# Position network: channels sorted by the sign of their last weight, four keys a group, half sums added by an accumulating DMA

## The chip, the cores and the metric

The kernel runs on one core of a Trainium2 chip. The core has a matrix engine (TensorE, PE in the profile; its weight loads are PEld), three other compute engines (VectorE, DVE; ScalarE, ACT; GpSimd, POOL), a sync engine (SP) and 16 DMA engines. Matmul results go to PSUM, everything else lives in SBUF (128 partitions) or in DRAM. All data are f32. The metric is the time of one execution on the device, in microseconds (us), median of several runs.

## The reference

Four layers follow each other on an image tensor; only the first is touched by the change, a deformable attention layer on x of shape (2, 512, 32, 32) with 8 heads. Its bias on the attention scores comes from a small network (the position network) that is evaluated for every pair of a query position (1024 of them) and a sampled key position (64 for each of 2 x 8 = 16 image and head pairs):

```python
pos = grid_q[:, :, None, :] - grid_kv[:, None, :, :]          # (16, 1024, 64, 2)
bias = jnp.sign(pos) * jnp.log1p(jnp.abs(pos))
bias = jax.nn.relu(bias @ cpb_w1 + cpb_b1)                    # 2 -> 128
bias = jax.nn.relu(bias @ cpb_w2 + cpb_b2)                    # 128 -> 128
bias = (bias @ cpb_w3 + cpb_b3).reshape(b, GROUPS, H * W, Hd * Wd)   # 128 -> 1
sim = jnp.einsum('bhid,bhjd->bhij', qh, kh) + bias
attn = jax.nn.softmax(sim, axis=-1)
out = jnp.einsum('bhij,bhjd->bhid', attn, vh)
```

The middle layer alone is 16 x 64 x 1024 columns through a 128 x 128 matrix. After this layer come an output projection, an MLP, a deformable convolution layer, a linear attention layer and a plain attention layer.

## The kernel before

The queries, keys and values are made first (`queries_keys_values`, L618 to L824): depthwise convolution of q on PE and DVE (L582, L591), the sampled positions, and the sampled features as matmuls (L788). Its results are q in a padded buffer that lies in a large buffer called room, the keys as two-head blocks `kbd`, and the signed logarithms of the distances, stored to DRAM as `feat`.

Then the position network runs (`biased_scores`, L827). The 16 image and head pairs go in eight steps of two (index p), each step over its keys. The hidden channels (128) stand on the partitions, the 1024 queries along the free dimension. The first layer is separable in x and y: `first_layer` (L510) loads the tables `ab` from `feat` by SP, and ACT scales them (L533). For a key, `hidden` adds a row of the x table and a column of the y table on DVE (L868) into a tile `h1` of 128x1024, and a ReLU follows in place, on ACT (L877) or, for 3 keys of 16, on DVE (L875). The pool of `h1` has six buffers.

The second layer goes by two keys (`second_layer`, L880). PE works in four column strips of 32: each of the two PSUM tiles `ph` gets 32 output channels of each key twice over, so that the lower 64 channels of both keys lie in the first tile and the upper 64 in the second. ACT evacuates the first with a ReLU (`lo`, L898), the second with a ReLU of the channels scaled by the size of their last weight (`hi`, L900); DVE adds `lo` times a signed quotient (`low_w`) to `hi` (L901). The last layer (L909) multiplies the sums by a matrix of signs, 128x32, that collects two keys; eight matmuls serve four pairs, and the result builds up in a PSUM tile `sim` over the 16 steps of a p. The scores q times k are added into the same PSUM tile by PE (`scores`, L921). `store` (L931) copies `sim` plus the last bias to the table simT. There are three PSUM tiles for `ph`.

PE's queue has the order of the program text. The queues of DVE, ACT, POOL and SP are put in order at build time by a scheduler that goes by the program text and by when it expects an operand; an engine executes its queue strictly in that order. An instruction waits for the semaphores of what it reads, and of the last readers of what it overwrites.

In the second half of the stage (p of 4 and more) the softmaxes of the first image's four steps are woven in (L1005 to L1032). The MLP's first weights (4 MB) and the output weights are loaded by SP in the middle of the last p (`load_weights`, L317), into the buffer that held q. After the stage come the projection (L1055, L1067) and the MLP (L1127, L1116).

Of the kernel before, what the change touches and what calls it, by code (L numbers as in the profile page):

```python
# [17 lines left out]
C = 512  # L18
CC = 4
HW = 1024  # L20
NP = 8
# [51 lines left out]
def constants():  # L73
    p = np.arange(128)
    px, py = (p % 32).astype(np.float32), (p // 32).astype(np.float32)
    neg_y = np.stack([-(py + 4.0 * c) for c in range(8)], axis=1).astype(np.float32)
    j = np.arange(64)
    gx, gy = (j % 8).astype(np.float32), (j // 8).astype(np.float32)

    gj = np.stack([gx, gy]).reshape(2, 1, 4, 16).repeat(16, axis=1)  # L80
    gj = gj.transpose(2, 0, 1, 3).reshape(128, 16)
    line = (2.0 * np.arange(32, dtype=np.float32) / np.float32(31) - 1.0).astype(np.float32)
    groups = np.zeros((128, 128), np.float32)
    for g in range(8):
        groups[16 * g : 16 * g + 16, 16 * g : 16 * g + 16] = 1.0 / 16

    y, x = np.divmod(np.arange(HW), 32)
    taps = np.zeros((HW, 9, 2), np.float32)
    for k in range(9):
        taps[:, k, 0] = y + k // 3 - 1  # L90
        taps[:, k, 1] = x + k % 3 - 1
    taps = taps.reshape(8, 128, 18).transpose(1, 0, 2).reshape(128, 144)
    parts = [
        ("ident", np.eye(128, dtype=np.float32)),
        ("groups", groups),
        ("minus", np.broadcast_to(np.array([0.0, -1.0], np.float32), (128, 2))),
        ("neg_xh", -px[:, None] - np.float32(0.5)),
        ("neg_yh", neg_y - np.float32(0.5)),
        ("gx", np.broadcast_to(gx, (128, 64))),
        ("gy", np.broadcast_to(gy, (128, 64))),  # L100
        ("gj", gj),
        ("line", np.broadcast_to(line, (128, 32))),
    ]
    packed, at = _pack(parts)
    return packed, at, taps


def layouts(i):
# [10 lines left out]
    for name in ("cpb_b2", "cpb_w3"):  # L119

        halves = np.asarray(i["L0_conv_" + name]).reshape(2, 64, 1)
        parts.append((name, np.concatenate([_twice(halves[0]), _twice(halves[1])], axis=1)))
# [20 lines left out]
    cst, cst_at, taps = constants()  # L143
# [8 lines left out]
    for h in range(2):  # L152
# [17 lines left out]
        "w2": np.asarray(i["L0_conv_cpb_w2"]),  # L170
# [106 lines left out]
def layers(net, out):  # L277
# [12 lines left out]
    with ExitStack() as later:  # L290
# [12 lines left out]
        with ExitStack() as l0a:  # L303
# [8 lines left out]
            w2 = keys.tile([128, 128], F32, name="w2_t", tag="w2")  # L312
            first = net.pool(l0a, "cpb_ab", 4)
            parts = queries_keys_values(net, bn, simT, q_flat, q_pad, kbd, val, feat, first)
            nc.sync.dma_start(out=w2, in_=net.ins["w2"])

            def load_weights():  # L317
                t = new_room()
                w1 = t[:, : 4 * 2048].rearrange("p (k m) -> p k m", m=2048)
                out_w = t[:, 4 * 2048 :].rearrange("p (k m) -> p k m", m=C)  # L320
                nc.sync.dma_start(out=out_w, in_=net.ins["out_w"])
                nc.sync.dma_start(out=w1, in_=net.ins["mlp_w1"])
                return w1, out_w

            w1, out_w = biased_scores(
                net, q_pad, kbd, feat, w2, simT, first, parts, load_weights
            )

# [289 lines left out]
def queries_keys_values(net, bn, simT, q_flat, q_pad, kbd, val, feat, first):  # L618
# [5 lines left out]
    with ExitStack() as ctx:  # L624
# [15 lines left out]
        with ExitStack() as part:  # L640
# [33 lines left out]

            pd = bank("pd")
# [6 lines left out]
            nc.scalar.activation(g, g, AF.Gelu, bias=net.vec("odw_b"))  # L682

        with ExitStack() as part:
# [61 lines left out]

            for gt, name in grids:
                g3 = gt.rearrange("p (n j) -> p n j", j=64)
                base = net.cst(name).unsqueeze(1).to_broadcast([128, NP, 64])
                nc.vector.scalar_tensor_tensor(g3, g3, 4.0, base, ALU.mult, ALU.add)  # L750
# [55 lines left out]
            for w, out, factor in ((kw, kbd, 64**-0.5), (vw, val, 1.0)):  # L806
                for q in range(2):
# [15 lines left out]
                    )  # L823
    return done  # L824


def biased_scores(net, q_pad, kbd, feat, w2, simT, first, parts, load_weights):  # L827
# [12 lines left out]
    with ExitStack() as ctx:  # L840
        small = net.pool(ctx, "cpb_w", 1)
        hid1 = net.pool(ctx, "cpb_h1", 6)
        lows = net.pool(ctx, "cpb_lo", 2)
        highs = net.pool(ctx, "cpb_hi", 6)
        ps_h = net.psum(ctx, "cpb_ps_h", 3)
        ps_sim = net.psum(ctx, "cpb_ps_sim", 1)
        w3_lo, w3_hi = net.vec("cpb_w3", 0), net.vec("cpb_w3", 1)
        b2_lo, b2_hi = net.vec("cpb_b2", 0), net.vec("cpb_b2", 1)
        sign = small.tile([128, 1], F32, name="sign", tag="sign")
        nc.vector.tensor_scalar(sign, w3_hi, 0.0, 2.0, ALU.is_ge, ALU.mult)  # L850
        nc.vector.tensor_scalar(sign, sign, 1.0, None, ALU.subtract)
        size = small.tile([128, 1], F32, name="size", tag="size")
        nc.vector.tensor_tensor(size, w3_hi, sign, ALU.mult)
        size_b = small.tile([128, 1], F32, name="size_b", tag="size_b")
        nc.vector.tensor_tensor(size_b, size, b2_hi, ALU.mult)
        low_w = small.tile([128, 1], F32, name="low_w", tag="low_w")
        nc.vector.tensor_tensor(low_w, w3_lo, sign, ALU.mult)

        w3 = small.tile([128, 62], F32, name="w3", tag="w3")
        nc.vector.memset(w3, 0.0)  # L860
        nc.vector.tensor_copy(w3[0:64, 30:31], sign[0:64, :])
        nc.vector.tensor_copy(w3[64:128, 31:32], sign[64:128, :])

        def hidden(i, j, on_vector):
            at_x, at_y = parts[i, j % 32 // 16]
            k = 16 * (j // 32) + j % 16
            h1 = hid1.tile([128, HW], F32, name="h1", tag="h1")
            nc.vector.tensor_tensor(  # L868
                h1.rearrange("p (y x) -> p y x", x=32),
                at_x[:, k : k + 1, :].to_broadcast([128, 32, 32]),  # L870
                at_y[:, k, :].unsqueeze(2).to_broadcast([128, 32, 32]),
                ALU.add,
            )
            if on_vector:
                nc.vector.tensor_scalar(h1, h1, 0.0, None, ALU.max)  # L875
            else:
                nc.scalar.activation(h1, h1, AF.Relu)  # L877
            return h1

        def second_layer(pair):  # L880

            phs = []
            for k in range(2):
                ph = ps_h.tile([128, HW], F32, name="ph", tag="ph")
                for n in range(2):
                    for t in range(4):
                        c0 = 64 * k + 32 * (t % 2)
                        nc.tensor.matmul(  # L888
                            ph[32 * t : 32 * t + 32, half(n)],
                            lhsT=w2[:, c0 : c0 + 32],  # L890
                            rhs=pair[t // 2][:, half(n)],
                            start=True,
                            stop=True,
                            skip_group_check=True,
                        )
                phs.append(ph)
            lo = lows.tile([128, HW], F32, name="lo", tag="lo")
            nc.scalar.activation(lo, phs[0], AF.Relu, bias=b2_lo)  # L898
            hi = highs.tile([128, HW], F32, name="hi", tag="hi")
            nc.scalar.activation(hi, phs[1], AF.Relu, bias=size_b, scale=size)  # L900
            nc.vector.scalar_tensor_tensor(hi, lo, low_w, hi, ALU.mult, ALU.add)  # L901
            return hi

        def last_layer(sim, j, sums):


            for n in range(2):
                for t in range(4):
                    nc.tensor.matmul(  # L909
                        sim[32 * t : 32 * t + 32, half(n)],  # L910
                        lhsT=w3[:, 30 - j : 62 - j],
                        rhs=sums[t][:, half(n)],
                        start=(j == 0),
                        stop=(j == 30),
                        skip_group_check=True,
                    )

        def scores(p, sim):
            for n in range(2):
                for t in range(2):  # L920
                    nc.tensor.matmul(  # L921
                        sim[64 * t : 64 * t + 64, half(n)].rearrange("p (y x) -> p y x", x=32),
                        lhsT=kbd[:, p, 64 * t : 64 * t + 64],
                        rhs=q_pad[:, p, 1 + 16 * n : 17 + 16 * n, 1:33],
                        start=False,
                        stop=False,
# [3 lines left out]
        def store(p, sim):  # L930
            nc.vector.tensor_scalar(simT[:, p, :], sim, net.vec("cpb_b3"), None, ALU.add)  # L931
# [16 lines left out]
        hidden_done = 0  # L948
        for p, j in [(p, j) for p in range(NP) for j in range(0, 32, 2)]:
# [5 lines left out]
            for t in range(4):  # L955
                pair = []
                for k in range(2):
                    key = j + 32 * (t % 2) + k
                    pair.append(hidden(2 * p + t // 2, key, hidden_done % 16 in (3, 8, 13)))
                    hidden_done += 1  # L960
                sums.append(second_layer(pair))
# [6 lines left out]
            elif j == 16:  # L968
                scores(p, sim)
                if p == NP - 1:  # L970
                    weights = load_weights()
# [7 lines left out]
        return weights  # L979
# [1184 lines left out]
```

## Time and profile before

| what | value |
|---|---|
| three runs | 3840.08, 3830.84, 3836.54 us, median 3836.54 |
| profiled execution, first to last instruction (the page gives no other time of it) | 3835.8 us |
| busy: PE, weight loads, DVE, ACT, POOL | 3739.0, 1487.3, 2765.5, 2566.4, 189.1 us |
| second layer of the position network (L888), first and last start | 86.6 and 2116.4 us |
| L888 matmuls, records | 16384, 593 ns each, 1808.0 us in all |
| ACT ReLU of h1 (L877); evacuations L898 and L900 | 872.1; 571.8 and 621.3 us |
| DVE first-layer sums (L868); additions (L901) | 1206.0; 654.8 us |

How to read it: an f32 matmul shows as two records; four of them run side by side in the four strips, so that the sum of their durations is four times the time they take. The mean of a group includes the end of the instruction that overlaps with the next one's start; the distance between the starts of two instructions that follow each other is shorter. Idle time of an engine counts only where that engine is what the others wait for.

### The profile page before, as it was taken

Reading aid. Unit: us, or ns where it says so; the run is one execution under the profiler, and the core shown is the slowest. Engines: PE = TensorE matmul, PEld = TensorE weight load, DVE = VectorE, ACT = ScalarE, POOL = GpSimd, SP = SyncE. Lnnn points to the kernel's source line nnn. Section 1 sums busy time; section 2 is a strip of 40 time slices with the busy share of each in tenths; the row PEclk is TensorE's granted clock in tenths of the full one; section 3 lists DMA queues with packets and bytes.
Section 4 is the critical chain, followed back from the end, with each engine's and each line's share of the span. In section 5 each row is a group of like instructions: output and inputs, shape, how many; then the busy total and the mean of one; then the engine's idle time right before and its main releaser. Section 6 shows DMA issues by size and latency. Waiting matters only on the chain. (4 is left out here: it accounts for less than half of the span.)

```text
span 3835.8 us, 59384 instructions
## 1 busy us (share of the span) xinstructions
PE 3739.0 (97%) x25356; PEld 1487.3 (39%) x25356; DVE 2765.5 (72%) x3242; ACT 2566.4 (67%) x2941; POOL 189.1 (5%) x180
## 2 busy tenths in 40 slices
PE   7999999999999999999999999999979999899999
PEld 4532222223222322232323444444434544455555
DVE  6999999999999999999999210411475472566565
ACT  7999999999999999999999221211123243345544
POOL 0000000000000000000000000000261150000000
PEclk9999999999999999999999999999999999999999
DMA  3000000000000000000000100112455481000000
GB/s 111 1 23 23 23 1 23 23 23 12 12 23 23 12 12 23 23 12 12 23 23 34 61 0 0 40 61 77 143 185 173 140 276 42 1 12 1 1 20 25
DMA packets 54459, 168.57 MB, mean 44 GB/s; under 512 B 4804, under 2 KB 10436, under 8 KB 51252
## 3 DMA queue, kind: packets, MB, share of 16 engines
q1 hardware_dynamic: 31556, 83.77, 6.2%
q0 software_dynamic: 21776, 79.14, 6.2%
q8 instruction: 200, 3.28, 0.4%
q10 hardware_dynamic: 864, 1.86, 0.2%
q14 instruction: 63, 0.52, 0.0%
HBM read 156.11 MB, written 8.65 MB: 43 GB/s over the span
## 5 line engine op out<-in xcount | busy, mean ns | idle before, releaser
L888 PE MATMUL ph<-h,w_t 128*32 128x512 f32 x16384 | 1808.0, 593 | 15.7 <-ACT lo L898 6.5
L868 DVE TENSOR_TENSOR h<-ab 128x1024 f32<-128x1024 f32 x1024 | 1206.0, 1219 | 67.2 <-PE ph L888 66.2
L888 PEld LDWEIGHTS ph<-h,w_t 128*32 128x32 f32 x16384 | 547.6, 110 | 1239.9 <-issue 1017.2
L877 ACT ACTIVATE h<-h 128x1024 f32<-128x1024 f32 x832 | 872.1, 1067 | 45.6 <-DVE h L868 42.9
L901 DVE SCALAR_TENSOR_TENSOR hi<-lo,low_w,hi 128x1024 f32<-128x1024 f32 x512 | 654.8, 1279 | 31.6 <-ACT hi L900 30.3
L900 ACT ACTIVATE hi<-ph,size_b,size 128x1024 f32<-128x1024 f32 x512 | 621.3, 1214 | 16.7 <-PE ph L888 12.5
L898 ACT ACTIVATE lo<-ph,vec_t 128x1024 f32<-128x1024 f32 x512 | 571.8, 1117 | 5.8 <-PE ph L888 5.4
L2086 ACT ACTIVATE e<-pl,m 128x1024 f32<-128x1024 f32 x128 | 143.6, 1122 | 228.9 <-DVE m L2078 228.9
L1567 PE MATMUL po<-fold,turned 128*128 128x512 f32 x576 | 266.1, 606 | 3.2 <-DVE dfacc L1575 2.9
L2078 DVE TENSOR_REDUCE m<-pl 128x1 f32<-128x1024 f32 x128 | 150.7, 1219 | 147.2 <-PE pl L1988 147.2
L1135 ACT ACTIVATE h<-ph,vec_t 128x512 f32<-128x512 f32 x64 | 44.0, 687 | 312.0 <-PE ph L1127 311.5
L909 PE MATMUL sim<-hi,w 128*32 128x512 f32 x2048 | 251.0, 592 | 0.0
L1127 PE MATMUL ph<-xn,room 128*128 128x512 f32 x512 | 230.9, 594 | 0.0
L1116 PE MATMUL acc<-h,mlp_w_t 128*128 128x512 f32 x512 | 229.8, 592 | 0.0
L1514 DVE SCALAR_TENSOR_TENSOR sum<-got,wts,sum 128x256 f32<-128x256 f32 x432 | 184.4, 478 | 48.8 <-ACT sum L1510 46.4
L1490 POOL DMA_INDIRECT got<-table,idx x144 | 175.0, 1215 | 554.9 <-DVE sum L1514 268.0
L2040 PE MATMUL pt<-cst_t,e 128*128 128x128 f32 x1024 | 149.3, 279 | 6.6 <-ACT aT L2051 4.0
L2040 PEld LDWEIGHTS pt<-cst_t,e 128*128 128x128 f32 x1024 | 118.6, 142 | 93.6 <-issue 61.3
L1567 PEld LDWEIGHTS po<-fold,turned 128*128 128x128 f32 x576 | 106.6, 195 | 112.4 <-issue 107.4
L1116 PEld LDWEIGHTS acc<-h,mlp_w_t 128*128 128x128 f32 x512 | 97.3, 190 | 122.5 <-issue 122.0
L1127 PEld LDWEIGHTS ph<-xn,room 128*128 128x128 f32 x512 | 96.6, 191 | 117.7 <-issue 117.1
L1541 ACT COPY turned<-pt 128x512 f32<-128x512 f32 x72 | 41.9, 582 | 143.8 <-PE pt L1535 143.6
(250 smaller groups left out, 2711.6 us busy)
## 6 DMA issues: line engine op xcount, KB each, us to landing
ab<-feat_d SPq DMA_DIRECT2D x64, 512.0 KB, 4.0
room<-in_dc_w_dram SPq DMA_DIRECT2D x9, 1024.0 KB, 4.8
dc_w_t<-in_dc_w_dram SPq DMA_DIRECT2D x5, 1024.0 KB, 5.3
room<-in_mlp_w_dram SPq DMA_DIRECT2D x1, 4096.0 KB, 15.6
mlp_w_t<-in_mlp_w_dram SPq DMA_DIRECT2D x1, 4096.0 KB, 12.5
dc_w_t<-in_dc_w_dram SPq DMA_DIRECT2D x8, 512.0 KB, 5.0
w_qkv_t<-in_w_qkv_dram SPq DMA_DIRECT2D x3, 1024.0 KB, 8.6
out_dram<-x_all SPq DMA_DIRECT2D x12, 256.0 KB, 2.0
```

The lines of the kernel that those rows point to most:

```text
L868: nc.vector.tensor_tensor(h1.rearrange("p (y x) -> p y x", x=32), at_x[:, k : k + 1, :].to_broadcast([128, 32, 32]), at_y[:, k, :].unsquee ...
L877: nc.scalar.activation(h1, h1, AF.Relu)
L888: nc.tensor.matmul(ph[32 * t : 32 * t + 32, half(n)], lhsT=w2[:, c0 : c0 + 32], rhs=pair[t // 2][:, half(n)], start=True, stop=True, skip_ ...
L898: nc.scalar.activation(lo, phs[0], AF.Relu, bias=b2_lo)
L900: nc.scalar.activation(hi, phs[1], AF.Relu, bias=size_b, scale=size)
L901: nc.vector.scalar_tensor_tensor(hi, lo, low_w, hi, ALU.mult, ALU.add)
L909: nc.tensor.matmul(sim[32 * t : 32 * t + 32, half(n)], lhsT=w3[:, 30 - j : 62 - j], rhs=sums[t][:, half(n)], start=(j == 0), stop=(j == 30 ...
L1116: nc.tensor.matmul(accs[oc], lhsT=self.w2[:, m, 128 * oc : 128 * oc + 128], rhs=hs[m], start=(m == 0), stop=(m == 15),)
L1127: nc.tensor.matmul(ph, lhsT=self.w1[:, k, 128 * m : 128 * m + 128], rhs=xn[:, k, :], start=(k == 0), stop=(k == CC - 1),)
L1514: nc.vector.scalar_tensor_tensor(t[:, q, :], g[:, s, :], w, t[:, q, :], ALU.mult, ALU.add)
L1567: nc.tensor.matmul(self.out, lhsT=turned[:, at : at + 128], rhs=self.folded.w[k][:, i, :], start=(k == 0 and i == 0), stop=(k == 8 and i = ...
L2040: nc.tensor.transpose(pt[:, 128 * c : 128 * c + 128], e[:, 128 * k : 128 * k + 128], ident)
```

## The change

The 128 channels of the second layer are sorted on the chip (class `Order`) by the sign of their last weight, into four quarters of 32, such that each lane's quarters can be combined with one sign per lane. The weights of the second layer are scaled by the size of the last weight and permuted by matmuls with 0/1 matrices; biases, signs and one constant are put in the same order. These are some 70 DVE instructions on single columns, mostly, a few tiny matmuls and two small loads.

`biased_scores` then works by four keys: `hidden` makes two keys at once (128x2048) in one of four places of the buffer room (the place of the MLP's weights, and of q before that); one ReLU pair in 16 is on DVE (L1021 of the changed kernel), the others on ACT (L1023). A PSUM tile holds one quarter of the channels for four keys. ACT evacuates three quarters (L1042), DVE adds the first two (L1051), and takes the fourth from PSUM while adding the third (L1055: max with the negative bias, the rest of the ReLU going into the constant). The second of these half sums is added to the first by an accumulating DMA from SBUF to SBUF on POOL's queue (L1056). The last layer takes four keys at once, so it runs half as often. The scores are computed for all p before the stage and stored in simT; `store` adds them. The output weights are loaded before the stage, the MLP's after it.

```diff
+            t = new_room()
+            w1 = t[:, : 4 * 2048].rearrange("p (k m) -> p k m", m=2048)
...
+            nc.sync.dma_start(out=out_w, in_=net.ins["out_w"])
+            biased_scores(net, feat, order, simT, first, parts, w1)
+            for k in range(4):
+                nc.sync.dma_start(out=w1[:, k, :], in_=net.ins["mlp_w1"][:, k, :])
...
+class Order:
...
+    def ranks(self, tmp, room, bank):
...
+        nc.vector.tensor_scalar(self.plus, w3, 0.0, None, ALU.is_ge)
...
+        nc.vector.tensor_scalar(self.turned, self.turned, size, None, ALU.mult)
...
+        for n, lhsT in enumerate((self.at[:, 128:256], self.ones)):
+            nc.tensor.matmul(pr[:, n : n + 1], lhsT=lhsT, rhs=self.plus, start=True, stop=True)
...
+    def places(self, pr):
...
+        scalar(
+            self.spread,
...
+            up,
+            None,
+            ALU.is_equal,
+        )
+
+    def put(self, bank):
...
+        nc.scalar.copy(self.w2, pw[:, :128])
...
+    def constant(self, bank):
...
@@ def queries_keys_values
+            ranks = order.ranks(w, val.rearrange("p n m -> p (n m)"), bank)
             pd = bank("pd")
...
+            order.places(ranks)
...
+            order.put(bank)
+            order.constant(bank)
...
+            for p in range(NP):
+                for n in range(2):
+                    pq = bank("pqk")
+                    for t in range(2):
+                        nc.tensor.matmul(
+                            pq[64 * t : 64 * t + 64, :].rearrange("p (y x) -> p y x", x=32),
+                            lhsT=kbd[:, p, 64 * t : 64 * t + 64],
+                            rhs=q_pad[:, p, 1 + 16 * n : 17 + 16 * n, 1:33],
...
+                    (nc.vector.tensor_copy, nc.scalar.copy)[n](simT[:, p, half(n)], pq)
...
@@ def biased_scores
-        hid1 = net.pool(ctx, "cpb_h1", 6)
-        lows = net.pool(ctx, "cpb_lo", 2)
-        highs = net.pool(ctx, "cpb_hi", 6)
+        lows = net.pool(ctx, "cpb_lo", 4)
+        adds = net.pool(ctx, "cpb_add", 3)
+        highs = net.pool(ctx, "cpb_hi", 7)
...
-        def hidden(i, j, on_vector):
+        def hidden(i, j, at, on_vector):
...
-            h1 = hid1.tile([128, HW], F32, name="h1", tag="h1")
+            h1 = room[:, at, :].rearrange("p (k i) -> p k i", k=2)
             nc.vector.tensor_tensor(
...
-        def second_layer(pair):
...
+        def quarter(quad, q):
+            ph = ps_h.tile([128, HW], F32, name="ph", tag="ph")
+            for n in range(2):
+                for t in range(4):
+                    nc.tensor.matmul(
+                        ph[32 * t : 32 * t + 32, half(n)],
+                        lhsT=order.w2[:, 32 * q : 32 * q + 32],
+                        rhs=quad[t][:, half(n)],
...
+        def rectified(ph, q):
+            t = lows.tile([128, HW], F32, name="lo", tag="lo")
+            nc.scalar.activation(t, ph, AF.Relu, bias=order.bias[:, q : q + 1])
+            return t
+
+        def second_layer(quad):
+            r0 = rectified(quarter(quad, 0), 0)
+            r1 = rectified(quarter(quad, 1), 1)
+            total = highs.tile([128, HW], F32, name="hi", tag="hi")
+            nc.vector.scalar_tensor_tensor(total, r0, order.low, r1, ALU.mult, ALU.add)
+            r2 = rectified(quarter(quad, 2), 2)
+            ph = quarter(quad, 3)
+            more = adds.tile([128, HW], F32, name="more", tag="more")
+            nc.vector.scalar_tensor_tensor(more, ph, order.floor, r2, ALU.max, ALU.add)
+            nc.gpsimd.dma_start(out=total, in_=more, accum_op=ALU.add)
+            return total
...
-        for p, j in [(p, j) for p in range(NP) for j in range(0, 32, 2)]:
+        for p, j in [(p, j) for p in range(NP) for j in range(0, 32, 4)]:
...
             for t in range(4):
-                pair = []
-                for k in range(2):
+                quad = []
+                for k in range(0, 4, 2):
                     key = j + 32 * (t % 2) + k
-                    pair.append(hidden(2 * p + t // 2, key, hidden_done % 16 in (3, 8, 13)))
-                    hidden_done += 1
-                sums.append(second_layer(pair))
+                    quad += hidden(2 * p + t // 2, key, pairs_done % 4, pairs_done % 16 == 7)
+                    pairs_done += 1
+                sums.append(second_layer(quad))
                 if t == 1 and pending is not None:
                     last_layer(sim, *pending[1:])
```

## The prediction

> **What bounds the kernel now.** I read the page first (busy shares, the 40 slices), then the busy time by stretches, then the groups of instructions inside the position network, then its order in time. In the slices the first 55% of the span has PE, DVE and ACT all at nine tenths. The line table puts the first L888 matmul at 86.6 us and the last at 2116.4 us: the position network holds 2030 of the 3835.8 us. A stretch from its middle (length, then busy time of PE, weight loads, DVE, ACT and POOL, granted clock, DMA share, GB/s), and its groups over 1000 us:
>
> ```profile
> 600.00:1000.00 400.00, 397.25 (x3664) 117.65 (x3660) 379.57 (x344) 389.85 (x382) 0.00 (x0) 1.00 0.05 17
> ```
>
> ```profile
> L888 PE MATMUL ph<-h,w_t 128*32 128x512 f32 x8071 | 890.0, 593 | 6.9 <-ACT lo L898 3.7 <-ACT hi L900 2.4 <-DVE h L875 0.8
> L868 DVE TENSOR_TENSOR h<-ab 128x1024 f32<-128x1024 f32 x506 | 596.0, 1219 | 31.0 <-PE ph L888 30.4
> L877 ACT ACTIVATE h<-h 128x1024 f32<-128x1024 f32 x411 | 430.9, 1068 | 21.7 <-DVE h L868 21.0
> L901 DVE SCALAR_TENSOR_TENSOR hi<-lo,low_w,hi 128x1024 f32<-128x1024 f32 x253 | 323.6, 1279 | 13.4 <-ACT hi L900 12.8
> ...
> L875 DVE TENSOR_SCALAR h<-h 128x1024 f32<-128x1024 f32 x94 | 64.5, 686 | 0.0
> L533 ACT ACTIVATE ab<-ab,vec_t 128x1024 f32<-128x1024 f32 x32 | 39.1, 1223 | 0.0
> ```
>
> The reader sees three engines within 5% of each other, none waiting long for another: PE waits 7 us in 1000. PE is the bound by a little. Its own pace comes from the order in time (start, duration, what):
>
> ```profile
> 1009.26 1.90 PE L909 MATMUL sim<-hi,w 128*32 128x512 f32 x16
> ...
> 2109.99 7.05 PE L888 MATMUL ph<-h,w_t 128*32 128x512 f32 x64
> ```
>
> 64 second-layer instructions (four column strips side by side) take 7.05 us less the last one's 0.17 us of drain: 6.88. Last-layer sixteens take 1.72 in the same way. 16384/64 x 6.88 = 1761, 2048/16 x 1.72 = 220, the scores (L921) 15.5, the transposes of the first four softmaxes (half of L1005 and L1027) 8.5: 2005 of the 2030 us. ACT's own pace, start to start, is in the same view:
>
> ```profile
> 1007.56 1.05 ACT L877 ACTIVATE h<-h 128x1024 f32<-128x1024 f32 x1
> 1008.50 1.11 ACT L898 ACTIVATE lo<-ph,vec_t 128x1024 f32<-128x1024 f32 x1
> 1009.51 1.05 ACT L877 ACTIVATE h<-h 128x1024 f32<-128x1024 f32 x1
> ```
>
> ReLU from SBUF 0.94 us, ReLU from PSUM 1.01 (I use 1.00).
>
> **The change, part by part.** I call four keys a quad (256 of them), its two h1 pairs a and b, its three ACT evacuations r0, r1, r2.
>
> *Removed.* Half the last layer: 110 us of PE. The scores leave the stage: 15 us. ACT evacuates three quarters of four (768 instructions for 1024, none with a scale, 1.00 each); DVE takes the fourth from PSUM while it adds (1279 ns, as L931 from PSUM), so DVE keeps 512 such additions.
>
> *Resized.* A 2048-wide instruction adds one more 1024 to the data time. DVE goes from 690 ns at 512 wide (L782) to 1219 at 1024, so 2048 is 2.28 us, 2.20 start to start. ACT copies from PSUM go from 588 (L658) to 1012 (L1032), 0.42 us for 512, so a 2048 ReLU is 0.94 + 0.85 = 1.79 start to start and 1.92 to its end. DVE ReLU goes from 420 (L764) to 686: 1.22. Per quad DVE has 2 x 2.20 + 2 x 1.20 + 1.14/8 = 6.94 us, ACT 15/8 x 1.79 + 3 x 1.00 + 0.26 (L533) = 6.62, PE 6.88 + 0.43 = 7.31. By sums alone PE would still bind, at 7.31 against 2030/256 = 7.93 now.
>
> *The wait that comes in.* Before, h1 has six buffers of one key, three groups of two; a group is made while two others are in use. Now the room holds four pairs, which is two quads: pair a of quad i+2 can be written only when PE has ended quad i. In the order in which the changed program is built, ACT's queue in 176 of the 256 quads stands r0(i), ReLU a(i+1), r1(i), r2(i), ReLU b(i+1), and only then r0(i+1). PE needs b for the third matmul of quad i+1, and r0(i+1) needs PE's first quarter of it. So the queue closes a ring. From PE's start on b of quad i: first quarter 4 x 0.43 plus drain 0.16 and hop 0.05 = 1.93; r0 1.00; ReLU a 1.79; r1 1.00; r2 1.00; ReLU b to its end 1.92; hop to PE 0.05. That is **8.7 us** (8.69; I take 8.74 with 0.05 for the semaphore instruction that stands before r0). The hops are from the order in time at the stage's start: an ACT h ended at 86.59 and PE started at 86.64; ph's last record ended at 91.72 and lo started at 91.76. PE has 6.88 in it, or 8.60 with a last layer: it waits 1.9 us in a normal quad. What stands behind the waiting r0 on ACT is the next ReLU a, which is ready 0.6 us after PE's start (DVE starts it when PE ends the quad before) and idles in the queue for 1.3 us. DVE is off the ring: b's sum is done 2.6 us before ACT takes it.
>
> In the other 80 quads (64 of them the third of a step's four quads, where ReLU a already stands ahead of r0 and DVE often does ReLU b; 10 first, 6 fourth) PE binds at 6.88. The last layer stands behind a step's second quad, where the ring has room for it. Sum: 176 x 8.74 + 80 x 6.88 = 2089. The 60 later L533 activations (1.13 each) and the first four softmaxes' ACT parts (13) are on the ring or in its 1.9 us gaps: 0 to 81, I take half, 41. Stage 2130: **+100**. Bounds on the ring: without the 0.05 and with half the drain, 8.6 (-25); with the 2048 ReLU at twice 0.94, 8.9 (+35).
>
> *Added ahead of the stage.* Scores for all p: 16 x 0.86 = 13.8 us of PE; their 16 PSUM copies (686 and 588 ns, DVE and ACT in turn) hide under it. The hidden pairs lie in the buffer that holds q, so the first ones wait for the last of these matmuls: 2.28 + 2.20 + 1.92 = 6.4 us to PE's first second-layer start, where it is 3.4 now (L888's idle at 86.64): +3. Some 70 one-column DVE instructions (153 ns for such a one at L851, less when queued) are 5 to 10 us of DVE, half woven between the 818 ns L591 steps, whose end PE waits for: 0 to 7, I take 2. Two small loads on SP stand ahead of nothing urgent; five tiny matmuls, 1 us. **+20**.
>
> *DMA.* 256 accumulating transfers of 512 KB on POOL's queue, idle now in this stage. The trace has none. Nearest rows (the last number is us to landing; a got is 128x1024, also 512 KB):
>
> ```profile
> ab<-feat_d SPq DMA_DIRECT2D x64, 512.0 KB, 4.0
> ...
> got<-table,idx POOLq DMA_INDIRECT x144, 5.3
> ...
> x_all<-in_x_dram POOLq DMA_DIRECT2D x4, 512.0 KB, 10.1
> ```
>
> 4.0 to 10.1 us to land; I take 5.3 to 7, the same queue and size without the rush of the start. The sum of a step's last quad is read by PE two quads later: DVE ends its second half 3.5 us after PE's quad, and PE comes to it after 8.74 + 8.74 = 17.5 at most, 15.6 with a cheap quad. So 12 us of cover; the "more" buffers (three) give 22. Cost nothing; gone above 12 us. A gain is excluded, since nothing else used the queue. SP's next in line: the weights of the MLP, now 4 x 1 MB after the stage's last read (15.6 us for 4 MB now), needed 40 us later (L1127 at 2156): hidden. At the stage's end the last sum goes by DMA before PE's last layer: 1.3 + 6 against 1.2 + 1.3 now: **+4**.
>
> The Trainium skill, SBUF - State Buffer, "two separate sides", warns that a POOL-issued DMA cannot write its descriptors while DVE runs a two-port instruction. If so, one of the 32 DVE ReLUs could hold one transfer by 1.2 us; no row here shows it, and the sum stays as it is.
>
> *Clock.* PE now pauses about 1 us in full and another 0.9 in part per quad. The trace, in stretches of 3.4 us, each pair one after another:
>
> ```profile
> 2770.90:2774.30 3.40, 1.44 (x5) 0.51 (x4) 2.36 (x6) 0.00 (x0) 1.46 (x2) 1.00 0.07 11
> 2774.30:2777.70 3.40, 3.40 (x9) 1.74 (x8) 0.66 (x3) 0.59 (x1) 0.41 (x1) 0.50 0.85 267
> ...
> 2849.40:2852.80 3.40, 1.91 (x7) 1.00 (x8) 3.40 (x6) 0.99 (x3) 2.83 (x1) 1.00 0.26 101
> 2852.80:2856.20 3.40, 3.40 (x12) 1.72 (x11) 3.40 (x8) 0.92 (x2) 3.40 (x1) 1.00 0.01 2
> ```
>
> With 1.44 us of PE work in 3.4 the clock fell to half; with 1.91 it stayed. The ring leaves at least 2.4 of 3.4: no cost. The skill's TensorE: Matmul & The Clock Gate, "Part 1", ties the fall to an idle window of about 3.4 us; here 2 us of pause were enough, so the row counts. By the page the sum would be the same.
>
> **Sum.** +100 + 20 + 4 = +124 on the 3835.8 us span, which is 0.7 under the median of 3836.5: **3961**.
>
> **Rivals.**
> - *Ring* (forecast): 3961, own range 3910 to 4020.
> - *PE stays the bound* (the other side). If ACT's ring closes within PE's 7.31, which needs ReLU a ahead of r0 in most quads, the stage is 2030 - 110 - 15 = 1905 and the whole 3836 - 125 + 24 = 3735. For it: the sums per engine, 6.94 and 6.62 under 7.31. Against: the queue order. It is faster below a mean quad of 7.84.
> - *Late sums.* If an accumulating transfer needs over 12 us (reading both sides), PE waits the rest once in each of 64 steps: at 15 us 3961 + 190 = 4150 if nothing absorbs it, half if the ring does. Against: 5.3 for the same size on this queue.
> - *Half clock.* If partly used strips count less, quarters of 3.44 us enter the ring: 176 x 1.7 = +300, 4260. Against: the pair of stretches above.
>
> **How the numbers follow.** No change is within 0.2% (7.7 us), about what a measurement of this kernel can tell. Ring 0.80, PE bound 0.08 (0.06 of it faster, 0.02 in between and unmeasurable), late sums 0.09, half clock 0.03. Slower: 0.92; same 0.02; faster 0.06. The range leaves out half clock, PE bound and the far end of late sums: 3895 to 4080.
>
> **What would show it.** The page after: PE's busy share of the stage down with ACT r0's line waiting for PE some 1.9 us in most quads, PE's second layer waiting for ACT's ReLU of the room; second-layer span near 2130 us; first second-layer matmul near 106 us; accumulating DMAs landing within 12 us; clock 1.00. It is wrong if PE's second layer runs without these waits, if the last layer waits for DMA, or if ACT's 2048 ReLU isn't 1.9 us.

## The result, and the profile after

The changed kernel takes 3989.8 us (median of four runs, 3987.9 to 3992.9) against 3835.7 for the kernel before: 1.0404 times, 95% interval 1.0389 to 1.0418. It is 154 us slower; 124 were forecast (3961, range 3895 to 4080). On the profiled executions, 3835.8 and 3989.4 us, the 154 us lie in three places, read from the first and last start of the second layer:

| | before | after | difference | forecast |
|---|---|---|---|---|
| start to first second-layer matmul | 86.6 | 102.1 | +15.5 | +20 |
| first to last second-layer matmul | 2029.8 | 2155.8 | +126.0 | +100 |
| from there to the end | 1719.4 | 1731.5 | +12.1 | +4 |

The stretch from 600 to 1000 us after (same columns as before: length, then busy time of PE, weight loads, DVE, ACT and POOL, granted clock, DMA share, GB/s), and the groups of instructions of the stage with all their waits:

```profile
600.00:1000.00 400.00, 365.11 (x3196) 132.92 (x3192) 332.45 (x196) 320.43 (x242) 40.38 (x47) 1.00 0.36 79
```

```profile
L1030 PE MATMUL ph<-room,w_t 128*32 128x512 f32 x16384 | 1901.7, 594 | 168.1 <-ACT room L1023 140.6 <-ACT lo L1042 25.6 <-DVE room L1021 1.2
L1014 DVE TENSOR_TENSOR room<-ab 128x2048 f32<-128x2048 f32 x512 | 1166.7, 2283 | 18.4 <-PE ph L1030 14.8 <-PE pqk L975 0.2
L1023 ACT ACTIVATE room<-room 128x2048 f32<-128x2048 f32 x480 | 916.2, 1909 | 44.1 <-DVE room L1014 43.5
L1042 ACT ACTIVATE lo<-ph,bias 128x1024 f32<-128x1024 f32 x768 | 831.2, 1109 | 348.3 <-PE ph L1030 342.0 <-ACT lo L1042 0.2
```

No engine is busy throughout any more: PE 365 us of 400 where it had 397, DVE 332 for 380, ACT 320 for 390. They wait for each other in a circle: PE for ACT's ReLU of the room (140.6 us), ACT's evacuations for PE (342.0 us in 203 waits, among 768 evacuations; 1.7 us each). PE's wait counts only its full stops; until pair b comes, it has pair a's matmuls to do, and they are done early. The order in time shows one round of the circle (start, duration, what, idle time before it):

```profile
1016.77 7.67 PE L1030 MATMUL ph<-room,w_t 128*32 128x512 f32 x64 [1.12 <-ACT room L1023]
1018.78 1.11 ACT L1042 ACTIVATE lo<-ph,bias 128x1024 f32<-128x1024 f32 x1 [2.07 <-PE ph L1030]
1019.80 1.90 ACT L1023 ACTIVATE room<-room 128x2048 f32<-128x2048 f32 x1
1021.60 2.11 ACT L1042 ACTIVATE lo<-ph,bias 128x1024 f32<-128x1024 f32 x2
1023.59 1.91 ACT L1023 ACTIVATE room<-room 128x2048 f32<-128x2048 f32 x1
1025.56 7.06 PE L1030 MATMUL ph<-room,w_t 128*32 128x512 f32 x60 [1.12 <-ACT room L1023]
```

PE starts on pair b at 1016.77. r0 starts 2.01 us later, ReLU a 1.02 after that, r1 1.80 after that; r1 and r2 together take 1.99 (the third ACT row holds both), ReLU b with the hop to PE 1.97. That makes 8.79 us from PE's start on b to its next one, where the prediction had 8.74. The next two sections show by experiments that this circle sets the time, and what of the 154 us it does not explain.

### The profile page after: what moved, and what is told of

Read it like the earlier page. It is cut to its first block, busy times and chain, and to the rows that moved or that the text cites. A ratio compares the mean times of both kernels' runs of the same rounds, so it can differ in the third digit from the quotient of the medians.

```text
span 3989.4 us, 56616 instructions
## 1 busy us (share of the span) xinstructions
PE 3737.2 (94%) x24348; PEld 1597.6 (40%) x24348; DVE 2667.3 (67%) x2629; ACT 2349.2 (59%) x2342; POOL 409.0 (10%) x436
## 5 line engine op out<-in xcount | busy, mean ns | idle before, releaser
L1030 PE MATMUL ph<-room,w_t 128*32 128x512 f32 x16384 | 1901.7, 594 | 168.1 <-ACT room L1023 140.6
L1030 PEld LDWEIGHTS ph<-room,w_t 128*32 128x32 f32 x16384 | 665.1, 110 | 1375.6 <-issue 791.1
L1014 DVE TENSOR_TENSOR room<-ab 128x2048 f32<-128x2048 f32 x512 | 1166.7, 2283 | 18.4 <-PE ph L1030 14.8
L1042 ACT ACTIVATE lo<-ph,bias 128x1024 f32<-128x1024 f32 x768 | 831.2, 1109 | 348.3 <-PE ph L1030 342.0
L1023 ACT ACTIVATE room<-room 128x2048 f32<-128x2048 f32 x480 | 916.2, 1909 | 44.1 <-DVE room L1014 43.5
L1051 DVE SCALAR_TENSOR_TENSOR hi<-lo,low 128x1024 f32<-128x1024 f32 x256 | 328.5, 1283 | 312.8 <-ACT lo L1042 312.7
L1056 POOL DMA_DIRECT2D hi<-more x256 | 220.0, 859 | 1998.3 <-DVE more L1055 1980.3
L1055 DVE SCALAR_TENSOR_TENSOR more<-ph,floor,lo 128x1024 f32<-128x1024 f32 x256 | 326.9, 1277 | 2.6 <-ACT lo L1042 1.5
L1064 PE MATMUL sim<-hi,w 128*32 128x512 f32 x1024 | 137.7, 597 | 7.4 <-DMA hi<-more 7.4
```

The source lines that it names most:

```text
L1014: nc.vector.tensor_tensor(h1.rearrange("p k (y x) -> p k y x", x=32), at_x[:, k : k + 2, :].unsqueeze(2).to_broadcast([128, 2, 32, 32]), a ...
L1030: nc.tensor.matmul(ph[32 * t : 32 * t + 32, half(n)], lhsT=order.w2[:, 32 * q : 32 * q + 32], rhs=quad[t][:, half(n)], start=True, stop=Tr ...
L1042: nc.scalar.activation(t, ph, AF.Relu, bias=order.bias[:, q : q + 1])
L1051: nc.vector.scalar_tensor_tensor(total, r0, order.low, r1, ALU.mult, ALU.add)
L1055: nc.vector.scalar_tensor_tensor(more, ph, order.floor, r2, ALU.max, ALU.add)
L1056: nc.gpsimd.dma_start(out=total, in_=more, accum_op=ALU.add)
```

## The experiments

One theory stood against three others. *Ring*: ACT's queue order over four pair places closes a circle, whose instructions add up to 8.8 us a quad. The others were *late sums* (the accumulating DMA, or what its traffic does to others), *too much work* for DVE or ACT, and *the wide instructions*. Each stage time below is last start less first start of the second layer in that run's profile.

**The same work in a better and in a worse order.** The first kernel only fixes ACT's order, so that r2 comes behind ReLU b; the second puts both ReLUs behind r2. Pair places, sums and DMA stay.

```diff
+            nxt = ahead(0)
             r1 = rectified(quarter(quad, 1), 1)
...
+            nxt += ahead(1)
             r2 = rectified(quarter(quad, 2), 2)
...
-                nc.scalar.activation(h1, h1, AF.Relu)
+                behind(lambda: nc.scalar.activation(h1, h1, AF.Relu))
```

Here `ahead(0)` and `ahead(1)` issue the h1 sums and ReLUs a and b of the next quad, and `behind` queues each ReLU and evacuation after the one issued before it. The second kernel has `nxt = ahead(0) + ahead(1)` after r2.

> The changed kernel with ACT's queue held in another order, the same work in the same four pair places: r0(i), ReLU a(i+1), r1(i), ReLU b(i+1), r2(i), r0(i+1); in the changed kernel ReLU b comes behind r2. Ring theory: r2 now fills the time in which ACT waited for PE's first quarter, and the ring loses one evacuation: 1.93 + 1.00 + 1.79 + 1.00 + 1.92 + 0.05 = 7.69 us from PE's start on b to its next start. 256 x 7.69 = 1969, and 41 to 80 for the L532 activations and softmax parts on the ring: stage 2010 to 2060 us where it is 2156 now, whole kernel 3845 to 3895 (1.002 to 1.015 of before). Rival, late sums or DVE as the cause: the order on ACT changes nothing of that, stage 2150, whole kernel 3985 to 3995.

> The changed kernel with ACT's queue held in a worse order, same work, same places: r0(i), r1(i), r2(i), ReLU a(i+1), ReLU b(i+1). Ring theory: r2 can't start before PE's third quarter is done, 3 x 1.72 + 0.21 = 5.37 us after PE's start on b; then r2 1.00, ReLU a 1.79, ReLU b 1.92, hop 0.05: 10.13 us a quad, less some 1.9 us in the 32 quads whose second pair is on DVE: 256 x 10.13 - 32 x 1.9 = 2532: stage 2500 to 2600, whole kernel 4330 to 4430 (1.13 to 1.155 of before). Rival, late sums or PE as the cause: the order on ACT doesn't matter, 3985 to 4000.

Measured: 3883.9 us (1.0126, 1.0109 to 1.0143) with a stage of 2057 us, and 4409.4 us (1.1495, 1.1476 to 1.1514) with a stage of 2578. Both are inside what the ring gave, 106 us below and 420 above the changed kernel, with the same instructions. The round of the better order, in time:

```profile
874.68 1.11 ACT L1051 ACTIVATE lo<-ph,bias 128x1024 f32<-128x1024 f32 x1
875.69 1.91 ACT L1023 ACTIVATE room<-room 128x2048 f32<-128x2048 f32 x1
877.50 1.10 ACT L1051 ACTIVATE lo<-ph,bias 128x1024 f32<-128x1024 f32 x1
878.49 1.91 ACT L1023 ACTIVATE room<-room 128x2048 f32<-128x2048 f32 x1
880.29 1.11 ACT L1051 ACTIVATE lo<-ph,bias 128x1024 f32<-128x1024 f32 x1
...
882.47 1.11 ACT L1051 ACTIVATE lo<-ph,bias 128x1024 f32<-128x1024 f32 x1 [1.07 <-PE ph L1039]
```

The fifth row is r2, now in the gap in which ACT used to wait; r0 comes again after 7.79 us (882.47 less 874.68; 7.69 expected). In the worse order all of PE's full stops in the second layer are waits for ACT's ReLU of the room:

```profile
L1039 PE MATMUL ph<-room,w_t 128*32 128x512 f32 x16384 | 2066.4, 600 | 423.8 <-ACT room L1023 423.8
```

The edit also moves DVE's first-layer sums in the program text. They are not behind the loss: ACT's ReLUs of the room waited for DVE 2.1 us in all in this run, where they waited 43.5 in the changed kernel.

**A fifth pair place.** The output weights leave the room until the stage is over, and h1 goes round in five places.

```diff
+            five = t.rearrange("p (k m) -> p k m", m=2048)
+            biased_scores(net, feat, order, simT, first, parts, five)
             nc.sync.dma_start(out=out_w, in_=net.ins["out_w"])
-            biased_scores(net, feat, order, simT, first, parts, w1)
...
-                    quad += hidden(2 * p + t // 2, key, pairs_done % 4, pairs_done % 16 == 7)
+                    quad += hidden(2 * p + t // 2, key, pairs_done % 5, pairs_done % 16 == 7)
```

> The changed kernel with five pair places for h1 in room in place of four; the fifth is the place of the output weights, which are then loaded after the stage (1 MB) and not before it. Nothing else is written differently. Ring theory: a ReLU of the quad after next can stand in the time in which ACT waited for PE's first quarter, so the ring opens and PE binds at 6.88 + 0.43 = 7.31 us a quad: 256 x 7.31 = 1871 plus up to 40 for the quads around the vector ReLU and the softmax parts: stage 1871 to 1911 where it is 2156, and 0 to 10 us more after the stage for the output weights: whole kernel 3705 to 3765 (0.966 to 0.982 of before). Rival, late sums: the place of h1 doesn't matter, stage near 2150. Rival, DVE or ACT short of time by itself (6.94 and 6.62 by sums, more if the instructions overlap less than I think): stage 2000 or more.

Measured: 3741.3 us, 0.9749 of before (0.9733 to 0.9766), stage 1910 us. The stretch from 600 to 1000 us and the second layer's waits:

```profile
600.00:1000.00 400.00, 396.34 (x3688) 118.93 (x3684) 381.43 (x226) 366.56 (x278) 47.49 (x55) 1.00 0.42 88
```

```profile
L1031 PE MATMUL ph<-room,w_t 128*32 128x512 f32 x16384 | 1784.4, 593 | 27.3 <-ACT lo L1043 19.1 <-ACT room L1024 4.8 <-DVE more L1056 3.2
```

PE is busy 396 of 400 us again, and its wait for the ReLU falls from 140.6 to 4.8. So the change's own arithmetic was right: half the last layer less is a gain, once PE is kept fed. The same work, in instructions just as wide, takes 1910 us here, so neither *too much work* nor *the wide instructions* can by itself be what makes it 2156. 1910 us lies at the upper end of what was expected (1871 to 1911).

**The fifth place, without its order.** The scheduler used the fifth place to put ReLU a of the quad after next behind r2. This kernel has the place, but holds ACT's queue to r0, ReLU a, r1, r2, ReLU b. Against the kernel with the better order, besides the load of the output weights after the stage:

```diff
-            nxt += ahead(1)
             r2 = rectified(quarter(quad, 2), 2)
+            nxt += ahead(1)
...
-            return hidden(2 * p + t // 2, key, done % 4, done % 16 == 7)
+            return hidden(2 * p + t // 2, key, done % 5, done % 16 == 7)
```

> Five places, but ACT's queue held in the order that most quads of the changed kernel have: r0(i), ReLU a(i+1), r1(i), r2(i), ReLU b(i+1), r0(i+1). It tells the place apart from what is done with it. Theory that the ring is closed by ACT's order, and the place only allows another one: the ring is back at the 8.79 us that the changed kernel shows, in all quads but the 32 whose second pair is on DVE (8.79 - 1.9 = 6.9): 224 x 8.79 + 32 x 6.9 = 2190, and up to 80 for the L533 activations: stage 2170 to 2270, whole kernel 4000 to 4100 (1.043 to 1.069 of before). Rival, the fifth place by itself ends the wait: stage 1910, whole kernel 3738 to 3760.

Measured: 4014.8 us (1.047, 1.0452 to 1.0487), stage 2181. The ring is back at 8.73 to 8.79 us from r0 to r0 in ordinary quads and 6.87 in those with a DVE ReLU, and so is PE's wait:

```profile
L1040 PE MATMUL ph<-room,w_t 128*32 128x512 f32 x16384 | 1908.0, 594 | 202.1 <-ACT room L1024 200.4 <-ACT lo L1052 1.5
```

The place alone is worth nothing; what it permits in ACT's order is worth 273 us.

**Fewer buffers in the kernel before.** The change's one number that the ring blames, put alone into the old kernel: two groups share the h1 buffers.

```diff
-        hid1 = net.pool(ctx, "cpb_h1", 6)
+        hid1 = net.pool(ctx, "cpb_h1", 4)
```

> The kernel before with one number changed: four h1 buffers of one key in place of six, so that two groups share the buffers, as in the changed kernel (there a group is four keys, here two). It does the disputed thing alone: no sorting, no DMA, no wide instructions. Theory that the room's depth in groups costs by itself: a group's h1 can be started only when PE begins the group before it, 1.22 + 1.14 + 1.06 = 3.4 us of DVE and ACT then follow each other, and an evacuation of 1.0 to 1.1 often stands between them in ACT's queue, 4.4 us a group where it is 3.97: 512 x 0.43 = +220 us, bounds +50 and +500: whole kernel 3885 to 4340 (1.013 to 1.13 of before). Rival, the depth is not what costs in the changed kernel but the wide instructions or the DMA: PE stays the bound here and the time stays at 3830 to 3845.

Measured: 4059.9 us (1.0585, 1.0569 to 1.0602), stage 2257, 4.41 us a group. PE's wait is again for the ReLU:

```profile
L888 PE MATMUL ph<-h,w_t 128*32 128x512 f32 x16384 | 2002.9, 594 | 138.4 <-ACT h L877 132.6 <-DVE h L875 1.9
```

Depth in groups costs by itself, without the wide instructions and without the DMA.

**The accumulating DMA.** Three kernels ask what it costs. Two leave it out, one in the changed kernel and one with five places; the third keeps the sum and makes DVE do it, with five places.

```diff
-            nc.gpsimd.dma_start(out=total, in_=more, accum_op=ALU.add)
```

```diff
-            nc.gpsimd.dma_start(out=total, in_=more, accum_op=ALU.add)
+            nc.vector.tensor_tensor(total, total, more, ALU.add)
```

> The changed kernel without the accumulating DMA: the second half sums are computed as before but not added, so the bias misses two quarters of the hidden channels. Ring theory: the DMA lies beside the ring, the stage stays at 2150 to 2160 us; the 7 us that the last layer waits for the last sum at the end of the stage go, and a few of the late ab loads: whole kernel 3970 to 3985 (1.035 to 1.039 of before). Rival, late sums (the transfers, or what they do to other transfers, set the pace): the stage falls toward PE's 1871 to 1911, whole kernel 3735 to 3790.

> Five places, without the accumulating DMA: the second half sums are computed but not added, so the bias misses two quarters of the hidden channels. It asks what the DMA costs where PE binds. Theory, it lies beside PE: the stage stays at 1905 to 1910 us, and only the wait of the last layer at the end goes (4.7 us, and up to 8 more of the late output weights): whole kernel 3727 to 3740 (0.971 to 0.975 of before). Rival, the transfers cost PE something in every step: stage 1880 to 1890, whole kernel 3700 to 3720.

> The kernel with five places, all second half sums added by DVE (1.28 us, 1.20 start to start) in place of the accumulating DMA: what the DMA is worth once the ring is open. DVE then has 6.94 + 1.20 = 8.14 us a quad against PE's 7.31 and binds: 256 x 8.14 = 2084 and up to 60 more: stage 2084 to 2145 where it is 1910 with the DMA, whole kernel 3905 to 3980 (1.018 to 1.037 of before). Rival, DVE isn't short of time in this stage, and the DMA buys nothing: 3735 to 3760.

Measured: without the DMA 3960.3 us in the changed kernel (1.0325, 1.0308 to 1.0342; stage 2145.7), 3730.9 with five places (0.9727, 0.9711 to 0.9743; stage 1911.6); with DVE's sum 3976.3 (1.0369, 1.0354 to 1.0385; stage 2157). With the ring open the DMA costs the stage nothing (1910.0 with, 1911.6 without). In the changed kernel it costs 10 us of stage and more at the end than I expected (in the profiles 14 us between the last second-layer start and the projection, and 10 behind that): 29 us in all by the medians, where 5 to 20 were expected. What goes with the stage's 10 us can be seen at the activations of the `ab` tables, in the changed kernel and then without the DMA:

```profile
L532 ACT ACTIVATE ab<-ab,vec_t 128x1024 f32<-128x1024 f32 x64 | 76.1, 1195 | 24.0 <-DMA ab<-feat_d 23.5
```

```profile
L532 ACT ACTIVATE ab<-ab,vec_t 128x1024 f32<-128x1024 f32 x64 | 75.9, 1195 | 8.2 <-DMA ab<-feat_d 7.7
```

ACT waits 23.5 us for these loads against 7.7, and ACT is on the ring. The waits differ by more than the stage does, so how much of the 10 us is theirs is not shown. DVE's sum makes DVE the bound (the third busy time):

```profile
600.00:1000.00 400.00, 370.49 (x3270) 126.65 (x3265) 391.15 (x249) 326.21 (x248) 0.00 (x0) 0.99 0.05 17
```

The stage is 247 us longer than with the DMA (174 to 235 expected; DVE has 8.24 us of work a quad instead of the 8.14 I added up, 391/400 of 2157/256).

**The end of the stage.** The last two half sums go to DVE.

```diff
+            if late:
+                nc.vector.tensor_tensor(total, total, more, ALU.add)
+            else:
+                nc.gpsimd.dma_start(out=total, in_=more, accum_op=ALU.add)
...
+                sums.append(second_layer(quad, pairs_done > 512 - 3))
```

> The changed kernel with the second half sums of the last two quads of all added by DVE (1.28 us each) and not by DMA. In the changed kernel the last accumulating DMA is issued at 2260.1 us and lands at 2270.8, beside the four 1 MB loads of the MLP's weights that start at 2251, and PE waits 7.4 us for it. Theory that this wait is the end of the stage's path: the last layer ends some 10 us earlier, the second layer keeps its 2156 us: whole kernel 3976 to 3983 (1.036 to 1.039 of before). Rival, the projection is held by something else (the weights, the store): 3987 to 3992.

Measured: 3977.0 us (1.0366, 1.0351 to 1.0382), 12.8 us less than the changed kernel; stage 2157.1. The changed kernel first, then this one:

```profile
2251.19 7.93 SPq L326 DMA_DIRECT2D room<-in_mlp_w_dram  x4
...
2260.12 0.85 POOL L1056 DMA_DIRECT2D hi<-more  x1 [5.48 <-DVE more L1055]
...
2270.77 3.62 PE L1064 MATMUL sim<-hi,w 128*32 128x512 f32 x10 [5.22 <-DMA hi<-more]
```

```profile
2262.51 1.23 DVE L1057 TENSOR_TENSOR hi<-hi,more 128x1024 f32<-128x1024 f32 x1
...
2264.27 1.90 PE L1067 MATMUL sim<-hi,w 128*32 128x512 f32 x10
```

The last transfer takes 10.6 us to be of use to PE, beside 4 MB of weights that SP starts 9 us ahead of it; DVE's addition lets PE go on 0.5 us after it ends. No run moved the weight loads away: that they slowed the transfer is argued, not shown.

**Both together.** Five places, the last seven pairs (its expectation says eight) in four of them so that the output weights load during the stage, and the last two sums on DVE:

```diff
+        def place(n):
+
+            return n % 5 if n < 505 else (n - 505) % 4
...
+                if pairs_done == 506:
+                    load_out()
```

> The kernel with five places, and both ends of the stage's tail mended: the last eight pairs go round in four places only, so that the output weights are loaded to the fifth while the stage still runs, and the second half sums of the last two quads are added by DVE. In the kernel with five places PE's projection starts 18.0 us after the last second-layer start (8.2 in the kernel before), behind a wait of 4.7 us for the last DMA and the late output weights. Expected: the projection 8 to 9 us after it, the stage at 1910 to 1915: whole kernel 3728 to 3736 (0.972 to 0.974 of before). Rival, the tail is held by something else: 3738 to 3745.

Measured: 3732.8 us, 0.9729 of before (0.9716 to 0.9742), stage 1914, projection (L1067 of the kernel before) 8.4 us after the last second-layer start. It beats both kernels: 103 us below before, 257 below the changed one.

## Why the prediction was right, and where its sizes were off

*The ring* was right, in mechanism and in size: 8.79 us for 8.74 (with the order that the program has), 7.79 for 7.69 in the better order, and the better and worse order, the fifth place and its undoing moved the time as the sum of its terms says. In a clean round ACT's r0 waits 2.07 us where 1.9 was said.

*The stage* came out 26 us longer than the forecast 2130. Of this some 9 us is the ring itself: a clean step of four quads, as about half of them are, takes 33.24 us from r0 to r0 (8.79, 9.29, 6.37, 8.79) where the prediction's 3 x 8.74 + 6.88 gives 33.10, 0.14 x 64. The second quad takes 9.29, because there ReLU a of the quad after next already stands ahead of r0 and waits for DVE (0.75 us); the third gives it back. Ten more go with the accumulating DMA, by the run without it (2145.7 for 2155.8); the later `ab` loads are what the trace shows of them. The prediction's 41 us for the L533 activations and the softmaxes had a price for the activation, none for its wait for the load. Some 7 us are left that no run assigns.

*DMA, cost nothing*: half right. The sums do not come late in the steps: with the ring open, the stage is the same with and without them, and the late sums rival falls. The transfers land in 4.4 us, inside the bounds of 4.0 to 10.1 and below the 5.3 to 7 I took:

```profile
hi<-more POOLq DMA_DIRECT2D x256, 512.0 KB, 4.4
ab<-feat_d SPq DMA_DIRECT2D x64, 512.0 KB, 5.2
room<-in_mlp_w_dram SPq DMA_DIRECT2D x4, 1024.0 KB, 7.4
```

But the step looked only at who reads the sums, and not at the other transfers: the `ab` loads went from 4.0 to 5.2 us and became late on ACT, and the stage without the sums is 10 us shorter. That the loads are late because they share the way with the sums is not shown (last section).

*The tail, +4* failed as a size: +12.1. Its sum 1.3 + 6 against 1.2 + 1.3, which is 4.8 and not 4, took the quiet landing time. I had listed SP's weight loads as hidden, by when they are needed, and not asked what they do to the transfer beside them: it took 10.6 us. With DVE's addition the projection starts 8.4 us after the last second-layer start, as before (8.2), against 20.8.

*Setup, +20* came out at +15.5, from three rows: the copy that ends the sampled features is 0.5 us later than before (78.55 for 78.07; the small DVE instructions and tiny matmuls were priced at 3), the scores take 14.0 (13.8 forecast), and the first second-layer matmul waits 4.39 us where it waited 3.38.

```profile
83.66 14.02 PE L975 MATMUL pqk<-room,kbd 128*64 128x512 f32 x64
102.07 1.92 PE L1030 MATMUL ph<-room,w_t 128*32 128x512 f32 x4 [4.39 <-ACT room L1023]
```

I had let PE wait for the second ReLU (6.4 us); it starts with the first pair's matmuls.

*Clock and rivals.* From 200 to 2200 us the clock was 1.00 in every stretch, and the half clock rival falls. PE's full stops there are mostly 1.1 us, the longest 2.8. The Trainium skill, TensorE: Matmul & The Clock Gate, "Part 1", ties a fall to an idle window; PE's full stops here, shorter than the 3.4 us that the prediction gives for it, are no such window. The prediction's own row, where 2 us of pause were followed by half clock, doesn't fit that window, and the measurement decides. But the prediction's dividing line (a fall at 1.44 us of PE work in 3.4, none at 1.91) isn't a rule for every stretch either. Around the longest stop the changed kernel has 0.71 us of work, and the clock stayed:

```profile
1718.00:1721.40 3.40, 0.71 (x8) 0.29 (x12) 1.78 (x1) 3.40 (x4) 0.74 (x1) 1.00 0.68 136
1721.40:1724.80 3.40, 3.40 (x33) 1.19 (x26) 1.32 (x2) 3.40 (x4) 0.00 (x0) 1.00 0.10 19
```

Cut 1.4 us later, a stretch of the same length has 2.11 us of work. So "no cost" came out, but the step that led there was weaker than it looked: it rested on a few stretches, and what they show depends on where they are cut.

*PE stays the bound* falls for the changed kernel and is what five places show: 3741 against the 3735 worked out for it.

## What to carry to other kernels

Sums per engine say what a stage could take; the order of the queues over the buffers says what it takes. When a change makes the group larger and keeps the bytes, count the depth in groups, and follow one round of the circle (engine to engine until the same instruction of the next group) through each in-order queue: here it was forecast at 8.7 us and measured at 8.8, beside sums of 7.3. A place more can pay far beyond its size, but only through the instruction that it lets stand in the gap; and a transfer called hidden has to be checked against the transfers that run beside it, too.

## What the runs showed of the hardware

- An accumulating transfer of 512 KB from SBUF to SBUF landed in 4.4 us (median of 256), near a load of that size from DRAM (4.0 before the change). Beside four 1 MB loads the last one took 10.6.
- It cost the issuing engine 0.86 us an issue. With the ring open it cost the stage nothing (1910.0 us with it, 1911.6 without), while DVE's additions in its place made the stage 247 us longer.
- The `ab` loads landed in 5.2 us beside the sums in the changed kernel and in 4.7 without them. With five places they landed in 3.9 with the sums and in 4.6 without, and in 5.4 with the sums and ACT's held order. Sharing the way with the sums therefore does not explain these times; what does was not tried.
- From the start of the projection to the end, where nothing was changed, the profiles lie between 1701 and 1711 us. The run without the DMA has 1701, the changed kernel and the kernel before 1711; these 10 us are part of what that run gained, and their cause stays open.
